# Spreading ScalarE's steps and S's products over each block, and one scratch row for the search, in a graph-attention and nucleus-diffusion kernel

## The chip, the cores and the metric

The kernel runs on one core of a Trainium2 chip. The metric is the device time of one execution in microseconds, as the median over several executions. A core has five engines with a queue each, which run their instructions in the order of the queue and wait for each other by semaphores: PE (TensorE, matrix products), ACT (ScalarE), DVE (VectorE), POOL (GpSimd) and SP (SyncE, which here only issues DMAs).

## The reference, cut to what matters

There are N = 2708 nodes with 512 features each, and a 0/1 adjacency matrix. Layer 0 is a graph attention layer; layer 1 is a diffusion with two steps. Nearly all that the change touches is in layer 1:

```python
S = S + eye(n)                                     # S is the adjacency
Rf = S / clip(S.sum(axis=1, keepdims=True), 1e-12)
Rb = S / clip(S.sum(axis=0), 1e-12)[:, None]
Xf, Xb, Xa = X, X, X
for s in range(2):
    logits = (Xa @ W1) @ W2 @ (Xa @ W3).T          # 2708 x 2708
    A = softmax(logits, with all but the largest entries that
                together hold 0.9 of the row's softmax set to -inf)
    Xf = Rf @ Xf;  Xb = Rb @ Xb;  Xa = A @ Xa
    Z = Z + (Xf @ U1[s] + Xb @ U2[s] + Xa @ U3[s])
Y = X + Z
out = x + (Y - mean) / sqrt(var + 1e-5) * gamma + beta
```

So each step s needs, for every row, a threshold ("nucleus"): the smallest set of largest probabilities that holds 0.9 of the mass. Then come a product of the sparse matrix A with Xa, two products with S, three small products with U1, U2 and U3, and, after the second step, a layer norm of each row.

## The kernel before, in words

**Tiles and blocks.** The 2708 rows are 22 tiles of 128 (the last has 20). Layer 1 goes through them in pairs of tiles (`pairs`, 11 of them, NP = 11). The main loop (L1295 to L1421) runs for each step s over g = -1 to 10; one pass of it is called a block here. Within a block three pairs are in work: pair g is multiplied (PE), pair g+1 is searched for its threshold (DVE), and the logits of pair g+2 are made and exponentiated (PE, ACT). The order on PE, ACT, DVE and SP is the order in which the Python code emits (`tc.manual_schedule`, L1293); nothing is reordered on those four.

**What a block emits, in order.**
1. `lg[g+2].products()` (L510): 24 products of queries and keys in six column chunks per tile, each chunk copied from PSUM into the row buffer `p` by ACT (L520). The PSUM pool `ps_t` has two buffers, so PE can be two chunks ahead of ACT.
2. `search(lg[g+1], ...)` (L594), first half: DVE finds a threshold by rounds of "sum of all p at or above th" (L625, two per round; 2 rounds for s = 0, 4 for s = 1). It starts from sums at three guessed points, `pts`, which ACT and POOL have prepared (next paragraph, `masses`), read at L642.
3. `early()` (L1351), called after the first round: it has DVE take the row maxima `nmx` of pair g+2 (L545), and it fills the list `fills`, steps for ACT that will be handed out later.
4. `late()` (L1359): the PE work of pair g. `diffused` loads what the S products of earlier blocks made. `attended` (L1090) computes A @ Xa in 12 steps, six per tile: PE turns four 128x128 pieces of the kept row `keep[i]` (L1101), ACT copies them out (`at`, L1105), PE multiplies them with the values `va` (L1120). After a tile's last step ACT scales the result into `xa` (L1128). `mixed` (L1139) does the three products with U1, U2, U3 in 12 steps k (L1156, a load of `u_k` each), and `last()` (L1163) copies the two results into `yo` (ACT, L1168), loads `xw` from y_d (SP, L1171) and adds (POOL, L1172).
5. `finish` (L789), the last part of the search of pair g+1: for each of the two tiles DVE writes p below the threshold into `keep[i]` (L796), takes the 8 largest (L798), for s = 1 does both again for the next 8; then it computes the exact cut, writes the kept row into `keep[i]` (`kept_from` L721 for s = 0, `kept_ranked` L726 to L729 for s = 1) and branches on whether ties need more work (L880).

`keep` has two buffers (pool `wide`, L604), one per tile: those that finish(g+1) writes are those that `attended` of pair g reads. So DVE waits at L796 until PE has turned the last piece of that tile.

**The two lists that are handed out in between.** `fills` holds ACT's steps for pair g+2 (`Logits.exp`, L523): `root` and `full` for each tile (two passes of ACT over a row of 2708, L550 and L557), `points` (POOL works out the three guessed points, L562 to L572, and ACT negates them, L569), 12 `look` steps (a pass of ACT over a row each, L550), and `masses` (POOL, L575 to L577). For s = 1 the steps of the layer norm of the pair before (`normed_aside`, L1194) are in the same list: two `mean`, two `spread` (ACT, L1208, and three small POOL operations, L1219 to L1221) and two `ended` (ACT L1208, POOL L1227 and L1228, and a store of `yo` to `out` from POOL's queue, L1229). There are 18 steps for s = 0 and 24 for s = 1.

`others` holds the next products with S (class `Products`, L941). A step is one row block: SP loads `hl` (512 KB) and `s_r` (256 KB) into three buffers each (L971, L973), PE does 8 products (L981 for s = 0, L998 for s = 1). Every 22 such steps are followed by four (`scaled`, L984, or `stored`, L1001) in which ACT copies a result out and issues its store. A block takes 11 or 12 steps for s = 0 and 26 for s = 1 (22 and four `stored`).

**When they are handed out.** `paced(steps, n)` runs the next n of a list. Before the change `attended` runs, from its fourth step on, 2 fills per step up to the ninth and then 1 for s = 0, and 1 per step for the first tile and 2 for the second for s = 1; it runs all of `others` (1 per step) for s = 0, but for s = 1 only 3, in the last steps. `mixed` spreads the remaining `others` over its 12 steps (for s = 1 about 2 each), and takes one fill in six of its steps. What is left of `fills` is run at the end of the block (L1406).

Of the kernel before, what the change touches and what calls it, by code (L numbers as in the profile page):

```python
# [15 lines left out]
OP = mybir.AluOpType  # L16
# [37 lines left out]
def kernel(  # L54
# [25 lines left out]
    KD = D // P  # L80
    NT = -(-N // P)
# [9 lines left out]
    G = 2  # L91
# [502 lines left out]
    def search(lg, looked, early, late):  # L594
# [4 lines left out]
        v = nc.vector  # L599
# [189 lines left out]
        def finish(go):  # L789


            for i, pr in tiles:
                t, m = th[:pr, i:i + 1], kept[:pr, 1, i:i + 1]
                for e in range(0, nx, 8):
                    vs, ss = vn[:pr, i, e:e + 8], sn[:pr, i, e:e + 8]
                    v.scalar_tensor_tensor(keep[i][:pr], ps_[i][:pr], t, ps_[i][:pr], op0=OP.is_lt, op1=OP.mult,  # L796
                                           accum_out=left[:pr, i:i + 1] if e else None)
                    v.max(vs, keep[i][:pr])  # L798
                    if e:
                        m = left[:pr, i:i + 1]  # L800
                        v.tensor_tensor(m, tot[:pr, i:i + 1], m, op=OP.subtract)
                    v.tensor_tensor_scan(ss, vs, vs, m, OP.add, OP.bypass)
                    t = vn[:pr, i, e + 7:e + 8]
            rest = small.tile([P, G, max(NEXT)], F32, name="rest", bufs=1)[:, :, :nx]
            if lg.rank is not None:
                v.tensor_tensor(rest, sn, vn, op=OP.subtract)
                v.tensor_tensor(rest, rest, thr.unsqueeze(2).to_broadcast([P, G, nx]), op=OP.is_lt)
                v.memset(rest[:, :, 0], 1.0)
                v.scalar_tensor_tensor(rest, rest, 0.0, vn, op0=OP.is_equal, op1=OP.add)
                v.tensor_reduce(cut, rest, axis=AX.X, op=OP.min)  # L810

                v.tensor_tensor(rest, vn, cut.unsqueeze(2).to_broadcast([P, G, nx]), op=OP.is_gt)
                v.tensor_mul(rest, rest, sn)
                v.tensor_reduce(top, rest, axis=AX.X, op=OP.max)
                v.tensor_tensor(top, top, kept[:, 1], op=OP.max)
                v.reciprocal(one, cut)
                v.tensor_tensor(room, thr, top, op=OP.subtract)
                v.tensor_mul(room, room, one)
                for x in tiles:
                    kept_ranked(*x)  # L820
                v.memset(flag, 0.0)
                v.tensor_tensor(fr, sn[:, :, nx - 1], thr, op=OP.is_lt)
                v.tensor_mul(fr, fr, thr)
                v.scalar_tensor_tensor(short, fr, 1.0 - 1e-5, den, op0=OP.mult, op1=OP.is_gt)


                v.tensor_scalar(room, room, 0.5, ROUND, op0=OP.add, op1=OP.add)
                v.tensor_scalar(room, room, ROUND, None, op0=OP.subtract)
                v.tensor_tensor(over, den, top, op=OP.subtract)
                v.tensor_mul(over, over, one)  # L830
                v.tensor_tensor(over, over, room, op=OP.subtract)
                v.tensor_mul(over, over, over)
                v.tensor_scalar(over, over, 0.25, None, op0=OP.is_gt)
                return branch(go)
            v.tensor_tensor(fr, sn[:, :, nx - 1], thr, op=OP.is_lt)
            v.tensor_mul(fr, fr, thr)
            v.tensor_tensor(sn, sn, vn, op=OP.subtract)
            v.tensor_tensor(sn, sn, thr.unsqueeze(2).to_broadcast([P, G, nx]), op=OP.is_lt)
            v.memset(sn[:, :, 0], 1.0)

            v.scalar_tensor_tensor(rest, sn, 0.0, vn, op0=OP.is_equal, op1=OP.mult)
            v.scalar_tensor_tensor(sn, sn, 0.0, vn, op0=OP.is_equal, op1=OP.add)
            v.tensor_reduce(cut, sn, axis=AX.X, op=OP.min)
            v.tensor_tensor(rest, rest, cut.unsqueeze(2).to_broadcast([P, G, nx]), op=OP.is_equal)
            v.tensor_reduce(tied, rest, axis=AX.X, op=OP.max)
            for x in tiles:
                kept_from(*x)
            v.memset(flag, 0.0)


            v.scalar_tensor_tensor(short, fr, 1.0 - 1e-5, den, op0=OP.mult, op1=OP.is_gt)
            eighths = vn[:, :, 7:nx:8]
            v.tensor_tensor(eighth, eighths, cut.unsqueeze(2).to_broadcast([P, G, nx // 8]), op=OP.is_equal)
            v.tensor_reduce(fr, eighth, axis=AX.X, op=OP.max)
            v.tensor_scalar(fr, fr, -1e-5, 1.0 + 1e-5, op0=OP.mult, op1=OP.add)
            v.tensor_mul(fr, fr, thr)
            v.tensor_tensor(over, den, cut, op=OP.subtract)
            v.tensor_tensor(over, over, fr, op=OP.is_ge)
            v.tensor_tensor(over, over, tied, op=OP.max)
            branch(go)  # L860
# [41 lines left out]
    with ExitStack() as st:  # L902
# [134 lines left out]
        def paced(steps, n):  # L1037
            for step in steps[:n]:
                step()
            del steps[:n]  # L1040
# [49 lines left out]
        def attended(s, grp, keep, rden, fills, others, then):  # L1090

            def turned(i, t, cs):
                pr = rows[t]
                pt = ps_t.tile([P, TG, P], F32, name="t")
                at = work.tile([P, TG, P], F32, name="at")
                for j, c in enumerate(cs):  # L1100
                    nc.tensor.transpose(pt[:rows[c], j, :pr], keep[i][:pr, cols[c]], ident[:pr, :pr])  # L1101
                full = sum(rows[c] == P for c in cs)
                for r, j0, j1 in ((P, 0, full), (rows[cs[-1]], full, len(cs))):
                    if j0 < j1:
                        nc.scalar.copy(at[:r, j0:j1, :pr], pt[:r, j0:j1, :pr])  # L1105
                return at

            steps = [(i, t, cs) for i, t in enumerate(grp) for cs in tgroups]
            at = turned(*steps[0])
            xa = []  # L1110
            total = len(others)
            for n, (i, t, cs) in enumerate(steps):
                pr = rows[t]
                nxt = turned(*steps[n + 1]) if n + 1 < len(steps) else then()
                if n >= 3:
                    paced(fills, 1 + i if s else 1 if n > 8 else 2)
                if cs[0] == 0:
                    pa = ps_a.tile([P, D], F32, name="a")
                for j, c in enumerate(cs):
                    nc.tensor.matmul(pa[:pr], lhsT=at[:rows[c], j, :pr], rhs=va[:rows[c], c, :],  # L1120
                                     start=(c == 0), stop=(c == NT - 1))
                if not s:
                    paced(others, (total * (1 + i) + 23) // 24)
                elif i and cs[0] >= NT // 2 or len(grp) == 1:
                    paced(others, 1)
                if cs[-1] == NT - 1:
                    xa.append(work.tile([P, D], F32, name="xa"))
                    nc.scalar.activation(xa[i][:pr], pa[:pr], AF.Copy, scale=rden[:pr, i:i + 1])  # L1128
                    if not s:
                        nc.gpsimd.dma_start(out=xa_d[cols[t], :], in_=xa[i][:pr])  # L1130
                at = nxt
            return xa, at
# [6 lines left out]
        def mixed(s, grp, order, v, others, fills):  # L1139
# [5 lines left out]
            def part(n):  # L1145
# [6 lines left out]
                for k in range(KD):  # L1152
                    u_k = up.tile([P, D], F32, name="u_k")
                    nc.sync.dma_start(out=u_k, in_=u[s, k * P:(k + 1) * P, :])
                    for i, t in enumerate(grp):
                        nc.tensor.matmul(pz[i][:rows[t]], lhsT=v_t[:, k, i * P:i * P + rows[t]], rhs=u_k,  # L1156
                                         start=(n == 0 and k == 0), stop=(n == 2 and k == KD - 1))
                    paced(others, -(-len(others) // (3 * KD - n * KD - k)))
                    if n < 2 and k < 3:
                        paced(fills, 1)  # L1160
                return v_t

            def last():  # L1163
# [129 lines left out]
        with tc.manual_schedule(engines={PE, ACT, DVE, SP}):  # L1293
            rest_of_first = []
            for s in range(STEPS):  # L1295
# [37 lines left out]
                for g in range(-1, NP):  # L1333
# [15 lines left out]
                    others = S.take(n) if s or g < 0 else S.splitting(S.take(n), 9)  # L1349

                    def early(g=g):  # L1351
                        sums, squares, ends = normed_aside(norms) if norms else ([], [], [])
                        if g + 2 < NP:
                            steps = lg[g + 2].exp(between=ends)
                            fills.extend(sums + steps[:2] + squares + steps[2:])
                        else:
                            fills.extend(sums + squares + ends)

# [96 lines left out]
```

## Time and profile before

| | |
|---|---|
| runs of the kernel | 3882.49, 3883.42, 3888.15 us; median 3883.42 |
| the profiled execution's own time | 3880.74 us |
| its span, first to last instruction | 3878.8 us |
| blocks of s = 0 (g = 0 to 10), first product with A to the last with U | 1287 to 2412 us from the span's start |
| blocks of s = 1 | 2541 to 3868 us |
| busy in the block of s = 1 from 3179.6 to 3310.6 us (131.0 us) | PE 117.75, DVE 92.61, ACT 64.42, POOL 30.80 us |
| mean granted clock of PE over the span | 0.944 |

Times in the profile are from the span's start; "idle before, releaser" names what ended the idle time of an engine just before an instruction. A line such as "t L518 <- ACT p L520" says that L518 on PE, which writes t, waited for ACT's L520, which writes p. PE counts each of its fp32 products as two records, so an `attended` step shows as x8 at L1120 and an S step of s = 1 as x8 at L998 (which are single records). Layer 0 (to about 1090 us) and the preparation of each step are not touched by the change, apart from the block g = -1.

### The profile page before, as it was taken

How to read it: one execution, taken by the hardware profiler on the slowest of the kernel's cores; microseconds unless marked ns; L12 is line 12 of the kernel's file. 1: busy time of each engine (PE TensorE's matmuls, PEld its weight loads, DVE VectorE, ACT ScalarE, POOL GpSimd, SP SyncE). 2: the span in 40 equal slices, each digit the busy share in tenths (PEclk: the TensorE clock that was granted, in tenths of full speed). 3: DMA queues.
4: the chain of work that ended last, by engine and by line, in shares of the span. 5: the costliest groups of instructions: out<-in, count | busy, mean ns of one | idle time of the engine just before them, and what ended most of it. 6: DMA issues, size and time to landing. Idle time of an engine off the chain costs nothing. (4 is left out here: it accounts for less than half of the span.)

```text
span 3878.8 us, 35347 instructions
## 1 busy us (share of the span) xinstructions
PE 3419.4 (88%) x11058; PEld 1758.6 (45%) x11058; DVE 2634.8 (68%) x4749; ACT 1551.6 (40%) x2387; POOL 898.6 (23%) x1117
## 2 busy tenths in 40 slices
PE   8999999999766898989989897579898989898888
PEld 4333333334444454545544452445554555455543
DVE  4687898999852555556466525996598668766992
ACT  2343211111024655655556412463445444544521
POOL 4115142343310122122112212111123122212231
PEclk9999999999878899999989998889999999999999
DMA  3475423323068555445344453725754574457453
GB/s 112 159 262 203 146 101 118 99 86 111 36 201 293 193 203 202 151 145 177 128 159 163 159 162 112 256 83 195 251 182 149 179 255 165 143 203 246 164 182 110
DMA packets 296045, 644.28 MB, mean 166 GB/s; under 512 B 37804, under 2 KB 87614, under 8 KB 292828
## 3 DMA queue, kind: packets, MB, share of 16 engines
q1 hardware_dynamic: 262596, 550.73, 43.5%
q0 software_dynamic: 20176, 68.11, 4.5%
q10 hardware_dynamic: 13020, 22.63, 1.5%
q8 instruction: 89, 1.46, 0.2%
q14 instruction: 164, 1.34, 0.1%
HBM read 518.78 MB, written 122.57 MB: 165 GB/s over the span
## 5 line engine op out<-in xcount | busy, mean ns | idle before, releaser
L1120 PE MATMUL a<-va,at 128*128 128x512 f32 (+2 forms) x1936 | 910.3, 610 | 50.7 <-ACT at L1105 50.3
L426 PE MATMUL po<-e,fw 128*65 128x512 f32 (+4 forms) x2112 | 842.3, 555 | 29.9 <-DVE e L424 21.2
L424 DVE SCALAR_TENSOR_TENSOR e<-r_b,kk,a_c 128x512 f32<-128x512 f32 (+4 forms) x1056 | 751.1, 739 | 69.0 <-PE po L426 17.8
L550 ACT ACTIVATE junk_a<-p,nth 128x2708 uint8<-128x2708 f32 (+1 forms) x240 | 612.7, 2553 | 5.7 <-ACT xe L1004 0.8
L998 PE MATMUL q<-s_r,hl 128*128 128x512 f32 (+1 forms) x2112 | 549.6, 408 | 63.1 <-DMA s_r<-s_d 57.2
L1156 PE MATMUL a<-u_k,v_t 128*128 128x512 f32 (+1 forms) x1056 | 505.0, 614 | 53.5 <-ACT xa L1128 30.0
L1120 PEld LDWEIGHTS a<-va,at 128*128 128x128 f32 (+2 forms) x1936 | 344.4, 190 | 433.7 <-issue 353.4
L426 PEld LDWEIGHTS po<-e,fw 128*65 128x65 f32 (+1 forms) x2112 | 286.8, 140 | 545.6 <-issue 268.9
L998 PEld LDWEIGHTS q<-s_r,hl 128*128 128x128 f32 x2112 | 380.5, 193 | 232.5 <-issue 95.9
L625 DVE SCALAR_TENSOR_TENSOR junk<-p,th 128x2708 bf16<-128x2708 f32 (+1 forms) x132 | 405.2, 3069 | 4.3
L981 PE MATMUL q<-hl,s_r 128*128 128x512 f32 x968 | 284.1, 437 | 70.1 <-DMA s_r<-s_d 68.1
L1156 PEld LDWEIGHTS a<-u_k,v_t 128*128 128x128 f32 (+1 forms) x1056 | 190.1, 190 | 288.1 <-issue 199.5
L1105 ACT COPY at<-t 128x512 f32<-128x512 f32 (+3 forms) x308 | 139.9, 474 | 440.3 <-PE t L1101 432.9
L518 PE MATMUL t<-keys,q_t 128*128 128x452 f32 x528 | 175.6, 461 | 124.0 <-ACT p L520 102.9
L981 PEld LDWEIGHTS q<-hl,s_r 128*128 128x128 f32 x968 | 183.9, 194 | 161.6 <-issue 86.8
L796 DVE SCALAR_TENSOR_TENSOR keep<-p,th 128x2708 f32<-128x2708 f32 (+1 forms) x44 | 133.5, 3033 | 165.8 <-PE t L1101 164.7
L798 DVE MAX8 vn<-keep 128x8 f32<-128x2708 f32 (+1 forms) x66 | 196.8, 2981 | 2.3
L545 DVE TENSOR_REDUCE nmx<-p 128x1 f32<-128x2708 f32 (+1 forms) x44 | 129.8, 2968 | 86.2 <-ACT p L520 86.2
L518 PEld LDWEIGHTS t<-keys,q_t 128*128 128x128 f32 x528 | 96.4, 220 | 199.0 <-ACT p L520 162.6
L1172 POOL TENSOR_TENSOR yo<-yo,xw 128x512 f32<-128x512 f32 (+1 forms) x22 | 32.6, 1500 | 632.8 <-DMA xt_d<-xe 439.6
L408 ACT ACTIVATE s_c<-a_c 128x512 fp32r<-128x512 f32 (+3 forms) x132 | 76.2, 577 | 247.6 <-DMA a_c<-in_adj_t_dram 120.6
L520 ACT COPY p<-t 128x452 f32<-128x452 f32 (+2 forms) x264 | 134.3, 538 | 84.6 <-PE t L518 68.4
(319 smaller groups left out, 3377.6 us busy)
## 6 DMA issues: line engine op xcount, KB each, us to landing
s_r<-s_d SPq DMA_DIRECT2D x330, 256.0 KB
hl<-vhl_d SPq DMA_DIRECT2D x132, 512.0 KB
u_k<-in_L_gnn_U_dram SPq DMA_DIRECT2D x264, 256.0 KB
hl<-fhl_d SPq DMA_DIRECT2D x132, 512.0 KB
hl<-bhl_d SPq DMA_DIRECT2D x132, 512.0 KB
arow<-in_adj_dram SPq DMA_DIRECT2D x21, 1354.0 KB
s_d<-s_c SPq DMA_DIRECT2D x88, 256.0 KB
a_c<-in_adj_t_dram SPq DMA_DIRECT2D x84, 256.0 KB
```

What stands on the lines that cost most here:

```text
L424: nc.vector.scalar_tensor_tensor(e[:pr, :cw], r_b[:pr, i, :cw], kk[:pr, t, hd:hd + 1], a_c[t][:pr, :cw], op0=OP.max, op1=OP.mult)
L426: nc.tensor.matmul(po[i][:, :cw], lhsT=fw[:pr, t, hd, :], rhs=e[:pr, :cw], start=(t == 0), stop=(t == NT - 1))
L518: nc.tensor.matmul(pl[:, :c1 - c0], lhsT=q[:, i], rhs=self.keys[:, c0:c1], start=(i == 0), stop=(i == 1))
L520: nc.scalar.copy(p[:pr, c0:c1], pl[:pr, :c1 - c0])
L550: nc.scalar.activation(junk[:pr], self.p[i][:pr], func, **kw)
L625: v.scalar_tensor_tensor(junk_b[:pr], ps_[i][:pr], th, ps_[i][:pr], op0=OP.is_ge, op1=OP.mult, accum_out=dst)
L798: v.max(vs, keep[i][:pr])
L981: nc.tensor.matmul(self.half[j], lhsT=s_r[:, j * P:(j + 1) * P], rhs=hl[:, h], start=(c == 0 and h == 0), stop=(c == NT - 1 and h == 1))
L998: nc.tensor.matmul(self.half[k][:, :w], lhsT=hl[:, h, k * P:(k + 1) * P], rhs=s_r[:, :w], start=(c == 0 and h == 0), stop=(c == NT - 1 and ...
L1105: nc.scalar.copy(at[:r, j0:j1, :pr], pt[:r, j0:j1, :pr])
L1120: nc.tensor.matmul(pa[:pr], lhsT=at[:rows[c], j, :pr], rhs=va[:rows[c], c, :], start=(c == 0), stop=(c == NT - 1))
L1156: nc.tensor.matmul(pz[i][:rows[t]], lhsT=v_t[:, k, i * P:i * P + rows[t]], rhs=u_k, start=(n == 0 and k == 0), stop=(n == 2 and k == KD - 1))
```

## The change

Three things are changed.

- **One scratch row.** In `finish` the row of values below the threshold, which is only read by the `max` after it, goes into `keep[0]` for both tiles. The kept rows themselves are still written into `keep[i]` later.
- **S's products.** `attended` hands out one step of `others` after each of its 12 steps, for both s. For s = 0 that is what it did; for s = 1 it means 12 in `attended` and 14 in `mixed`, where it was 3 and 23.
- **ACT's steps.** `attended` hands out one fill per step from the third on (10 in all), `mixed` spreads the rest evenly over its 12 steps. The order in the list changes too: the two `mean` steps come after `points`, and `spread` and `ended` after `masses`, at the list's end. Where there is no norm to do (all blocks of s = 0, and the first of s = 1), two steps that do nothing stand in place of the two `mean` steps. In the block g = -1, which hands out one fill for every two steps of `others`, these empty steps take two of the turns.

```diff
@@ finish
-                    v.scalar_tensor_tensor(keep[i][:pr], ps_[i][:pr], t, ps_[i][:pr], op0=OP.is_lt, op1=OP.mult,
+                    v.scalar_tensor_tensor(keep[0][:pr], ps_[i][:pr], t, ps_[i][:pr], op0=OP.is_lt, op1=OP.mult,
                                            accum_out=left[:pr, i:i + 1] if e else None)
-                    v.max(vs, keep[i][:pr])
+                    v.max(vs, keep[0][:pr])
@@ attended
-            total = len(others)
             for n, (i, t, cs) in enumerate(steps):
                 pr = rows[t]
                 nxt = turned(*steps[n + 1]) if n + 1 < len(steps) else then()
-                if n >= 3:
-                    paced(fills, 1 + i if s else 1 if n > 8 else 2)
+                if n >= 2:
+                    paced(fills, 1)
...
-                if not s:
-                    paced(others, (total * (1 + i) + 23) // 24)
-                elif i and cs[0] >= NT // 2 or len(grp) == 1:
-                    paced(others, 1)
+                paced(others, 1)
@@ mixed
                     paced(others, -(-len(others) // (3 * KD - n * KD - k)))
-                    if n < 2 and k < 3:
-                        paced(fills, 1)
+                    paced(fills, -(-len(fills) // (3 * KD - n * KD - k)))
@@ early
-                        sums, squares, ends = normed_aside(norms) if norms else ([], [], [])
+                        sums, squares, ends = normed_aside(norms) if norms else ([lambda: None] * G, [], [])
                         if g + 2 < NP:
-                            steps = lg[g + 2].exp(between=ends)
-                            fills.extend(sums + steps[:2] + squares + steps[2:])
+                            fills.extend(lg[g + 2].exp(between=sums) + squares + ends)
                         else:
                             fills.extend(sums + squares + ends)
```

In the diff `sums`, `squares` and `ends` are the `mean`, `spread` and `ended` steps.

## The prediction, on record before the changed kernel ran

> **What bounds the kernel now.** I read the page first, then the waits of PE in the blocks of each step, then timelines of single blocks.
>
> ```profile
> span 3878.8 us, 35347 instructions
> PE 3419.4 (88%) x11058; PEld 1758.6 (45%) x11058; DVE 2634.8 (68%) x4749; ACT 1551.6 (40%) x2387; POOL 898.6 (23%) x1117
> ...
> PEclk9999999999878899999989998889999999999999
> ```
>
> PE is busy 88% of the span and no other engine comes near; what a change of order can win is PE's idle time and the slow clock that follows it. The waits of PE from 2600 to 3690 us (most of s = 1), and then from 1290 to 2190 us (s = 0); columns: total us, times, longest.
>
> ```profile
> PE t L518 <- ACT p L520: 52.9, 11, 8.4
> PE a L1120 <- ACT at L1105: 21.0, 10, 3.6
> PE a L1156 <- ACT xa L1128: 20.3, 9, 6.2
> PE q L998 <- DMA s_r<-s_d: 15.7, 25, 2.0
> ```
>
> ```profile
> PE a L1120 <- ACT at L1105: 23.0, 22, 5.5
> ...
> PE t L518 <- ACT p L520: 12.0, 40, 0.7
> PE a L1156 <- ACT xa L1128: 9.7, 8, 2.5
> PE a L1156 <- ACT v_t L1053: 3.6, 2, 2.0
> ```
>
> In both, PE waits for ACT copies, and ACT is late because of `fills` in front of them. The largest, L518, sits at the start of each block of s = 1. ACT and PE there:
>
> ```profile
> 3181.38 1.07 ACT L1168 COPY yo<-a 128x512 f32<-128x512 f32 x2 [0.47 <-PE t L518]
> 3182.34 2.56 ACT L550 ACTIVATE junk_a<-p,nth 128x2708 uint8<-128x2708 f32 x1
> ...
> 3185.03 2.55 ACT L550 ACTIVATE junk_a<-p,nth 128x2708 uint8<-128x2708 f32 x1
> ...
> 3187.58 0.95 ACT L520 COPY p<-t 128x452 f32<-128x452 f32 x2
> ```
>
> ```profile
> 3176.64 3.60 PE L1156 MATMUL a<-u_k,v_t 128*128 128x512 f32 x8
> 3179.67 1.38 PE L518 MATMUL t<-keys,q_t 128*128 128x452 f32 x4
> 3188.14 7.46 PE L518 MATMUL t<-keys,q_t 128*128 128x452 f32 x20 [7.10 <-ACT p L520]
> ```
>
> Two looks left over at the block's end (2.66 us each) hold the copies back until 8.0 us after E, the end of `mixed` (3179.6); PE idles 7.1 us. In the middle of the block:
>
> ```profile
> 3230.24 3.60 PE L1120 MATMUL a<-va,at 128*128 128x512 f32 x8
> 3239.10 5.40 PE L1120 MATMUL a<-va,at 128*128 128x512 f32 x8 [3.19 <-ACT at L1105]
> ```
>
> The same eight products take 5.40 us after the idle time and 3.60 before it; a window over 3239.3 to 3242.7 shows clock 0.50. So a stall of over 2 us costs itself and about 1.8 us more.
>
> **What the Trainium skill says.** "TensorE: Matmul & The Clock Gate", What's actually happening: after an idle window of some 3.4 us the array falls to half rate and is released again after such a window of work. The trace agrees in size (stretches of 0.50 of 3.4 us and multiples), though gaps of 2.5 us are enough here. The same page, Architectural detail: ACT's and DVE's queues are strictly first in, first out; the ACT timeline above shows it. "SBUF — State Buffer", SBUF: two separate sides: a DVE operation with two SBUF inputs and a POOL operation that reads SBUF exclude each other for the whole instruction. The trace agrees: POOL's power takes 0.56 us alone and 3.35 beside L625. "DMA: Bandwidth & Descriptors", Anatomy of one DMA: about 2.0 us plus bytes over 436 GB/s from POOL's queue, so an estimated 2.6 us for the 256 KB of `yo`; the profile's medians are 2.5 us (y_d) and 3.9 us (out), which I use.
>
> **The change, part by part.**
>
> *Scratch row.* DVE's wait at L796 goes away (about 26 us per block of s = 0), but DVE is not late there: no L1101 of s = 0 waits for it. The next thing late for DVE is `masses`. In s = 1 the S steps stretch `attended` from 12 x 3.87 to 12 x (3.87 + 1.84) = 68 us, so without the scratch row the second tile's L796 would have waited some 20 us; with it the first that needs the second buffer is L729, 39 us after the first L796 (3238.2 to 3277.3), by when the last piece is turned. I price it at nothing; the cover is some 30 us between finish and the next block's first L1101.
>
> *Stalls inside the blocks of s = 1.* With one fill (2.66) and one copy (0.58) ACT needs 3.2 us of each 5.7 us step; in `mixed` 9 looks (24 us) lie in 39 us. So the waits on `at` and `xa` go: 21.0 + 20.3, and one of 2.9 at 2573 us outside that window, 44 us. About ten of them exceed 2 us, with their slow clock 10 x 1.8 = 18 us.
>
> *S loads.* `mixed` before asks 2 x 768 KB + 256 KB per 5.4 us (about 330 GB/s) for ten of its steps, after for two. Of the L998 waits, 15.7 in the window and 5.5 after it, I take two thirds: 14 us.
>
> *The end of the block of s = 1.* The two looks go (5.3 us), and a new chain takes their place: `ended` are the last fills, and the copies into `yo` (ACT) now wait for the store of the old `yo`; behind them in ACT's queue stand the L520 copies, for which PE waits. Let T be the end of the last S step; four steps of `mixed` remain, 16 records, 6.9 us, so E = T + 6.9. ACT: copy and issue of `stored` 1.04, square 0.9: T + 1.95. POOL's three operations for it: 1.2 us alone, T + 3.2; if DVE's first two L625 lie there (E is 40 us after `attended` ends; six looks, the v_t copies that wait for PE's fifth step at 18.5, and three looks put masses at about E - 12; 4.8 us of DVE's small operations follow, so they probably do) until T + 7.1, the second tile's until T + 8.3. Then
>
> ```profile
> 3242.48 1.27 POOL L1228 TENSOR_TENSOR yo<-yo,xw 128x512 f32<-128x512 f32 x1
> 3243.71 1.28 POOL L1227 TENSOR_TENSOR yo<-yo,g_b 128x512 f32<-128x512 f32 x1
> 3244.94 0.67 POOL L1229 DMA_DIRECT2D out_dram<-yo  x1
> ```
>
> twice over: 2 x (1.25 + 1.25) and one issue (0.9) to the second store, whose landing takes 2.5. L520 starts at T + 15.0 (E + 8.1) if nothing meets DVE, at T + 17.8 (E + 10.9) if it does; 3.9 for the landing adds 1.4. I take E + 9.8 against E + 8.0: +1.8 us in the eight block starts g = 2 to 9, +14 us. Block g = 1 follows one without norms and wins 2 us.
>
> SP's queue: the `xw` loads from y_d now wait for POOL's L1228; behind them stand the q_t, xb_d, `scales`, `v_t`, `hl` and `s_r` loads. In the block shown `hl` is issued 4 us after the first xb_d load, and its bytes are down about 11 us after it; the first S product of the next `attended` comes 12.8 us after the first L520. The xb_d load moves with that L520, so about 2 us are left. Price: nothing, at most 3 us per block.
>
> *Last pairs.* From g = 8 on DVE decides: finish of pair 9, with ties, ended at 3698.4 and that of pair 10 at 3798.6. Earlier `masses` let DVE start some 8 us earlier, not 18 as PE would: I give back 9 us.
>
> *s = 0.* The 12 looks move from `attended` (2 per step) into `mixed`. Gone: 23.0 + 9.7 + 3.6 + 1.8, less 6.4 (seven `xa` waits of 0.9 that the last step's order keeps) and 3 (the `scaled` copies at 1720 to 1744): 28 us, and six slow-clock stretches, 11 us. New: after `xa` ACT has four looks, two v_t copies and five looks, 1.7 + 9 x 2.67 + 1.05 = 26.8 us after the end of `attended`, whereas PE is ready for the key copies (L162) after 23.9 and L518 needs what follows them. That is 2.9 us, 2.45 after the 0.45 that ACT idles there, and about 0.9 for the clock, nine times: 30 us. Net -9.
>
> *Blocks g = -1.* The empty fills leave two looks more behind ACT's last store: 5.3 us before L520 at 1276.6; at 2531.6 ACT waits 2.8 us for DVE anyway, so 2.6. Together +8.
>
> Sum: -44 - 18 - 14 + 14 - 2 + 9 - 9 + 8 = -56 us. Against the profiled execution: 3880.7 - 56 = 3825. The median of the runs is 3883.4, 2.7 higher: 3827. A difference under 0.2% (8 us) can't be told from no change here.
>
> **Rivals.** (B) The end chain is at its light end (-14) and the looks of s = 0 delay PE half as much (up to -16): 3797 to 3813. For it: DVE's passes may lie just before POOL's work. (C) Waits move without going: the chain at E + 12 to E + 14 (18 to 34 us over eight starts) and S loads up to 2 us late (16) give 3845 to 3876. For it: the median landing of `out` is 3.9, and POOL's L1227 and L1228 took 2.57 and 3.48 us where they met DVE. (D) Slower: the same chain beyond E + 16.8. Without it the sum is -70, over eight starts 8.8 us each, on top of the 8.0 of before; all four POOL operations meeting two-input DVE passes (3 us each, +7), with landings of 3.9, reach E + 19: some 3901. Against it: after the first round DVE reduces (L545, one input) or waits for `p`.
>
> **Chances.** Forecast 0.55 (3815 to 3845), B 0.17, C 0.18, D 0.10. The range 3800 to 3872 leaves out part of B and D. Faster by over 0.2% 0.85, within 0.06, slower 0.09.
>
> **What would show it.** In s = 1: no waits of L1120 on `at` over 1 us; L518 still waiting 6 to 10 us per block, now behind L1168 (the new line of L1168's copy) that waits for the `out` store; DVE's wait at L642 shorter. In s = 0: L162 released late, by ACT itself. Wrong if L518's wait vanishes or exceeds 12 us, if L998 waits at the start of `attended`, or if L1101 waits for DVE in the middle blocks.

## The result, and the profile after

The change gained nothing and cost a little: 3889.72 us median of 20 runs (3881.78 to 3899.36), against 3879.91 us of 20 runs of the kernel before (3870.74 to 3899.82). The ratio is 1.0024, 95% interval 1.0014 to 1.0035, so the kernel became 0.24% slower. The forecast was 3827.

The page after, the span, the busy times and the granted clock:

```profile
span 3880.0 us, 35402 instructions
...
PE 3388.3 (87%) x11058; PEld 1759.7 (45%) x11058; DVE 2655.2 (68%) x4749; ACT 1564.3 (40%) x2387; POOL 868.4 (22%) x1117
...
PEclk9999999999878898999999999889999999999989
```

PE is busy 31 us less than before with the same products, and the span is the same: PE idles that much more. The row of the clock hardly differs; the mean granted clock is 0.938, where it was 0.944. In such a case the page's totals don't say where to look, and the steps have to be compared one by one. Taking each step from its first product with A to its last with U:

| | before | after | forecast for the difference | measured |
|---|---|---|---|---|
| up to the first product of s = 0 and between the steps (g = -1) | 1287, 129 | 1295, 131 | +8 | +10 |
| s = 0 | 1125 | 1162 | -9 | +37 |
| s = 1 | 1327 | 1281 | -55 | -46 |

These sum to +1, and the two profiled spans differ by 1.2 us. The medians differ by 9.8 us; where the rest sits can't be read from one execution of each.

The waits of PE from 2640 to 3690 us after (s = 1; total us, times, longest):

```profile
PE t L518 <- ACT p L520: 78.1, 10, 11.4
PE q L999 <- DMA s_r<-s_d: 7.9, 3, 4.7
...
PE a L1120 <- ACT at L1106: 0.4, 2, 0.2
```

The waits for `at` and `xa` are gone, as forecast, those for S's loads (L999 is the old L998; 15.0 us before in the same window) are halved, and the wait of L518 at the start of each block has grown from 52.9 to 78.1. The end of one block of s = 1 (the old L1168 is L1164, the old L1229 is L1225). In this timeline and those below, lines that don't bear on the argument are left out:

```profile
3324.41 0.67 POOL L1225 DMA_DIRECT2D out_dram<-yo  x1 [0.30 <-POOL yo L1224]
3327.53 0.58 ACT L1164 COPY yo<-a 128x512 f32<-128x512 f32 x1 [4.62 <-DMA out_dram<-yo]
3328.01 0.58 POOL L1225 DMA_DIRECT2D out_dram<-yo  x1 [0.30 <-POOL yo L1224]
3331.21 0.58 ACT L1164 COPY yo<-a 128x512 f32<-128x512 f32 x1 [3.09 <-DMA out_dram<-yo]
3331.69 0.98 ACT L520 COPY p<-t 128x452 f32<-128x452 f32 x2
3332.28 4.24 PE L518 MATMUL t<-keys,q_t 128*128 128x452 f32 x9 [11.06 <-ACT p L520]
```

This is the chain that the prediction drew: each copy into `yo` waits for a store of the old `yo` (3.1 and 3.2 us from issue to release), and the key copies stand behind both. E, the end of L1153's last products, is 3320.4 here, so L520 starts at E + 11.3.

The waits of PE from 1290 to 2230 us (s = 0) are where the loss is:

```profile
PE q L982 <- DMA s_r<-s_d: 59.2, 7, 16.5
PE t L518 <- ACT kq_b L163: 12.0, 6, 2.4
PE a L1153 <- ACT xa L1125: 9.1, 8, 2.1
...
PE a L1120 <- ACT at L1106: 2.0, 5, 1.1
```

The line of L982 was this before:

```profile
PE q L981 <- DMA s_r<-s_d: 13.2, 5, 7.0
```

ACT's waits fell as forecast (L1120 from 23.8 to 2.0 in this window), the key copies are late by some 2 us a block, near the forecast's 2.45, and a wait that the prediction never mentions, for the loads of S's products, went from 13.2 us to 59.2. Where it comes from shows in one block, whose first L518 is at 1503.6:

```profile
1501.44 38.24 SPq L1025 DMA_DIRECT2D split_hl<-xfb_d  x2
1503.68 0.21 POOL L577 TENSOR_TENSOR pts<-signs,above 128x6 f32<-128x6 f32 x1
1512.44 3.04 DVE L625 SCALAR_TENSOR_TENSOR junk<-p,th 128x2708 bf16<-128x2708 f32 x1
1534.93 0.43 DVE L1013 TENSOR_SCALAR split_hl<-split_hl 128x512 int32<-128x512 int32 x1
1536.38 0.54 POOL L1016 DMA_DIRECT2D bhl_d<-split_hl  x1 [24.54 <-DVE split_hl L1015]
1539.74 0.68 SPq L972 DMA_DIRECT2D hl<-vhl_d  x1
1545.44 3.68 PE L982 MATMUL q<-hl,s_r 128*128 128x512 f32 x8 [16.50 <-DMA s_r<-s_d]
```

A function that the text so far left out is at work, `split` (L1009 to L1026). In s = 0 eight steps of `others` in each block also call it: DVE splits the oldest loaded rows into a high and a low part (L1013, L1015), POOL stores them (L1016), and SP loads the next rows into the same pool of two buffers (L1025). The load has to wait for the store of the buffer that it takes. Read the lines downwards: the looks end late, so the masses (L577) are there only at 1503.7; DVE's first round (L625) starts at 1512.4, and the splits, which stand behind both rounds in DVE's queue, at 1534.9; the store goes at 1536.4; and SP only then issues the `hl` and `s_r` loads queued behind it. (The first line covers two loads of L1025: one leaves at once, and the other stands for 37.5 us.) The `hl` and `s_r` loads have nothing to do with the split, and PE waits 16.5 us for them. In the same block before:

```profile
1462.23 0.20 POOL L577 TENSOR_TENSOR pts<-signs,above 128x6 f32<-128x6 f32 x1
...
1478.95 28.60 SPq L1024 DMA_DIRECT2D split_hl<-xfb_d  x2
...
1502.80 0.43 DVE L1012 TENSOR_SCALAR split_hl<-split_hl 128x512 int32<-128x512 int32 x1
...
1513.46 3.75 PE L981 MATMUL q<-hl,s_r 128*128 128x512 f32 x8 [7.01 <-DMA s_r<-s_d]
```

Here the block's L518 began at 1481.1, so the split came 21.7 us into it, against 31.4 after. The other blocks agree: before, the masses come 16 to 19 us ahead of the first L518 of a block, and after, in the eight blocks that follow g = 0, 0.1 to 0.3 us behind it; the first split moves from 21.7 to 31.4 or 31.5 us in five of seven. SP stood still before too, only 9 to 10 us less; most of that was covered by what had already been loaded.

### The profile page after: what moved, and what is told of

Read it like the earlier page. It is cut to its first block, busy times and chain, and to the rows that moved or that the text cites. A ratio compares the mean times of both kernels' runs of the same rounds, so it can differ in the third digit from the quotient of the medians.

```text
span 3880.0 us, 35402 instructions
## 1 busy us (share of the span) xinstructions
PE 3388.3 (87%) x11058; PEld 1759.7 (45%) x11058; DVE 2655.2 (68%) x4749; ACT 1564.3 (40%) x2387; POOL 868.4 (22%) x1117
## 4 chain that ended last, share of the span: by engine, by line
PE 45%; ACT 8%; DMA 8%; issue 5%; POOL 5%; DVE 1%; SPq 1%; ACTq 0%; POOLq 0%; DVEq 0%
PE a L1120 18%; PE q L999 11%; ACT junk_a L550 6%; PE a L1153 5%; PE q L982 5%; DMA s_r<-s_d 4%; PE t L518 3%; PE t L1102 2%; PE po L426 1%; DMA xfb_d<-xe 1%; POOL ln_sums L1216 1%; DMA out_dram<-yo 1%; ACT p L520 1%; DVE junk L625 1%; POOL ln_sums L1215 1%
## 5 line engine op out<-in xcount | busy, mean ns | idle before, releaser
L1120 PE MATMUL a<-va,at 128*128 128x512 f32 (+2 forms) x1936 | 893.9, 601 | 13.8 <-ACT at L1106 13.2
L999 PE MATMUL q<-s_r,hl 128*128 128x512 f32 (+1 forms) x2112 | 574.2, 416 | 61.1 <-DMA s_r<-s_d 55.6
L1153 PE MATMUL a<-u_k,v_t 128*128 128x512 f32 (+1 forms) x1056 | 491.5, 605 | 28.5 <-DMA u_k<-in_L_gnn_U_dram 18.0
L1120 PEld LDWEIGHTS a<-va,at 128*128 128x128 f32 (+2 forms) x1936 | 339.7, 188 | 382.3 <-issue 338.8
L999 PEld LDWEIGHTS q<-s_r,hl 128*128 128x128 f32 x2112 | 380.4, 191 | 245.3 <-issue 116.0
L625 DVE SCALAR_TENSOR_TENSOR junk<-p,th 128x2708 bf16<-128x2708 f32 (+1 forms) x132 | 402.8, 3052 | 4.3
L982 PE MATMUL q<-hl,s_r 128*128 128x512 f32 x968 | 287.9, 442 | 115.8 <-DMA s_r<-s_d 115.6
L518 PE MATMUL t<-keys,q_t 128*128 128x452 f32 x528 | 182.9, 479 | 167.4 <-ACT p L520 133.5
L1153 PEld LDWEIGHTS a<-u_k,v_t 128*128 128x128 f32 (+1 forms) x1056 | 189.0, 187 | 265.7 <-issue 201.6
L982 PEld LDWEIGHTS q<-hl,s_r 128*128 128x128 f32 x968 | 186.8, 197 | 209.1 <-issue 123.4
L545 DVE TENSOR_REDUCE nmx<-p 128x1 f32<-128x2708 f32 (+1 forms) x44 | 129.4, 2967 | 148.1 <-ACT p L520 148.1
L518 PEld LDWEIGHTS t<-keys,q_t 128*128 128x128 f32 x528 | 101.8, 230 | 245.4 <-ACT p L520 200.5
L642 DVE TENSOR_TENSOR pts<-top,pts 128x6 f32<-128x6 f32 x22 | 5.5, 251 | 276.8 <-POOL pts L577 276.8
L520 ACT COPY p<-t 128x452 f32<-128x452 f32 (+2 forms) x264 | 136.7, 539 | 84.6 <-PE t L518 68.7
L1102 PE MATMUL t<-ident,keep 128*128 128x128 f32 (+1 forms) x968 | 148.4, 274 | 15.6 <-DVE keep L748 11.4
```

The source lines that it names most:

```text
L518: nc.tensor.matmul(pl[:, :c1 - c0], lhsT=q[:, i], rhs=self.keys[:, c0:c1], start=(i == 0), stop=(i == 1))
L520: nc.scalar.copy(p[:pr, c0:c1], pl[:pr, :c1 - c0])
L625: v.scalar_tensor_tensor(junk_b[:pr], ps_[i][:pr], th, ps_[i][:pr], op0=OP.is_ge, op1=OP.mult, accum_out=dst)
L982: nc.tensor.matmul(self.half[j], lhsT=s_r[:, j * P:(j + 1) * P], rhs=hl[:, h], start=(c == 0 and h == 0), stop=(c == NT - 1 and h == 1))
L999: nc.tensor.matmul(self.half[k][:, :w], lhsT=hl[:, h, k * P:(k + 1) * P], rhs=s_r[:, :w], start=(c == 0 and h == 0), stop=(c == NT - 1 and ...
```

## The experiments

Ratios are to the kernel before, with 95% intervals; s = 0 and s = 1 are measured as in the table above (before 1125 and 1327, after 1162 and 1281).

**1. s = 0 as before.** The changed kernel, with the old places of the fills in s = 0:

```diff
@@ attended
-                if n >= 2:
-                    paced(fills, 1)
+                if n >= (2 if s else 3):
+                    paced(fills, 1 if s or n > 8 else 2)
@@ mixed
-                    paced(fills, -(-len(fills) // (3 * KD - n * KD - k)))
+                    if s:
+                        paced(fills, -(-len(fills) // (3 * KD - n * KD - k)))
+                    elif n < 2 and k < 3:
+                        paced(fills, 1)
@@ early
-    sums, squares, ends = normed_aside(norms) if norms else ([lambda: None] * G, [], [])
+    sums, squares, ends = normed_aside(norms) if norms else ([lambda: None] * G if s else [], [], [])
```

> The changed kernel with the fills of s = 0 placed as before (three steps late and up to two per step in attended, three in mixed, no empty steps); s = 1 and the scratch row stay as changed. Theory 1 (the loss is s = 0's late looks: masses late, DVE's splits late, SP's queue behind them): s = 0 falls from 1162 to about 1125 us again, the waits of L982 in it from 59 to under 20 us, the whole to 3835 to 3850, about 1% faster than before. Rival (s = 0 loses by the one scratch row or by what s = 1's changes do to the prologue and the loads): s = 0 stays near 1160 us and the whole near 3890.

3832.22 us, ratio 0.9877 (0.9858 to 0.9897). s = 0 took 1114 us, s = 1 1284, and L982's waits are back at 13.4 us. The loss is in s = 0 and in the places of its fills. (s = 0 is 11 us shorter than before; one L998 wait of 5.5 us near its end is missing. It may be the scratch row; this was not separated.)

**2. s = 0 alone.** The kernel before, with only s = 0's part of the change; in `early` the empty steps and the order of the list as well.

```diff
@@ attended
-                if n >= 3:
-                    paced(fills, 1 + i if s else 1 if n > 8 else 2)
+                if n >= (3 if s else 2):
+                    paced(fills, 1 + i if s else 1)
@@ mixed
-                    if n < 2 and k < 3:
+                    if not s:
+                        paced(fills, -(-len(fills) // (3 * KD - n * KD - k)))
+                    elif n < 2 and k < 3:
                         paced(fills, 1)
```

> The kernel before with the new places of s = 0's fills alone (spread over attended and mixed, and the empty steps); s = 1 and two scratch rows as before. Theory 1: s = 0 loses 35 to 45 us by itself, with 5 more in the block g = -1: 3920 to 3935, about 1.1% slower than before. Rival (the loss needs the one scratch row or s = 1's part): within 10 us of before, 3875 to 3893.

3928.36 us, ratio 1.0123 (1.0105 to 1.0141); s = 0 1166 us, L981's waits 58.4 us. The loss needs neither the scratch row nor s = 1.

**3. The split's load from POOL's queue.** The changed kernel with

```diff
@@ split
-                    nc.sync.dma_start(out=hl[:pr, 1], in_=xfb_d[i, cols[t], :])
+                    nc.gpsimd.dma_start(out=hl[:pr, 1], in_=xfb_d[i, cols[t], :])
```

> The changed kernel, only that the load of the split's second half is issued from POOL's queue and no longer from SP's, so that SP's loads of keys and factors need not stand behind a split that DVE has not finished. Theory 1 with SP's queue as the last link: the waits of L982 on s_r in s = 0 fall from 59 us to under 20, and s = 0 by 30 to 45 us, the whole to 3845 to 3860. Rival (the products of S wait because the split's own parts come late, not because SP is blocked; then it does not matter who issues the load): L982 keeps some 50 to 60 us of waits and the time stays within 10 us of 3890.

3819.18 us, ratio 0.9848 (0.9831 to 0.9865), better than expected: s = 0 took 1093 us, 69 less than in the changed kernel and 32 less than before. The waits of PE from 1290 to 2230 us in this kernel:

```profile
PE a L1120 <- ACT at L1106: 15.1, 10, 6.3
PE t L518 <- ACT kq_b L163: 11.6, 7, 2.4
PE a L1153 <- ACT xa L1125: 9.8, 8, 2.5
```

No L982 wait is listed, although masses and splits are as late as in the changed kernel (in the block with L518 from 1490.1, the split is at 1521.6, 31.5 us into it). So the products did not need what was late; SP's queue was the link. What the new key-copy delay costs is seen undisturbed here: 12 us of waits, where the forecast's 30 had 22 of waits (nine of 2.45) and 8 of slow clock.

**4. Norm steps before the looks.** The changed kernel with

```diff
@@ early
-                            fills.extend(lg[g + 2].exp(between=sums) + squares + ends)
+                            fills.extend(lg[g + 2].exp(between=sums + squares + ends))
```

> The changed kernel, only that squares and ends of the norms stand directly behind the sums among the fills of s = 1 and the last looks come after them. Theory 2 (what is left of the wait of L518 in s = 1, 78 us from 2640 to 3690, is the chain store of yo, POOL, ACT's copy at the block's end): the waits of L518 there fall under 30 us and s = 1 by 35 to 60 us, the whole to 3830 to 3855. Rival (the looks at the end take its place, as in the kernel before where two left-over looks held the copies 8.0 us): L518 keeps 60 us or more and the time stays within 15 us of 3890; a third way, masses come later and DVE decides the blocks of s = 1, would show DVE waits at L1102 and a time above 3890.

3850.64 us, ratio 0.9932 (0.9914 to 0.995); s = 1 fell to 1243 us and L518's waits to 31.7 us, 4.2 per block. The chain over the store of `yo` was the residue in s = 1; what now ends the wait is the last look, still on ACT when the block ends.

**5. Both edits**, the diffs of runs 3 and 4, on the changed kernel.

> The changed kernel with both edits that each helped: the split's second load issued from POOL's queue (alone it gave 3819) and squares and ends directly behind the sums (alone 3851, that is 39 us under the changed kernel). If the two causes are separate, one in s = 0 and one in s = 1, the gains add: 3819 - 39 = 3780, range 3772 to 3790, about 2.6% faster than before. If they share a wait (POOL's queue, which then carries both the split's loads and the norms' work), half of the second gain is lost: 3795 to 3815.

3780.8 us, ratio 0.974 (0.9727 to 0.9753); s = 0 1091, s = 1 1242. The two causes are separate and add up.

**6. The split's load from POOL's queue in the kernel before**, the diff of run 3.

> The kernel before, only that the split's second load is issued from POOL's queue. Theory (SP's queue behind DVE's split is a cost in the kernel before too, but a small one: 13.2 us of L981 and 5.5 of L998 waits from 1290 to 2230 us, with slow clock after them): s = 0 wins 15 to 25 us, the whole 3858 to 3868, so that the new fills' own cost in s = 0, with SP freed, would be near nothing. Rival 1 (the late looks cost s = 0 by ACT as well, by the predicted 30 us, and the freed SP merely hides that): the kernel before wins as much from this edit as the changed one did, 60 to 75 us, to 3808 to 3823. Rival 2 (SP's blocks are covered in the kernel before): 3878 to 3888.

3879.1 us, ratio 0.9994 (0.9985 to 1.0003): no gain, the time that the second rival gave. The profile does not show it as cover, though: L981's wait on `s_r` is gone here too (13.2 us before), and L1120's wait for ACT rose from 23.8 to 44.8 us, the longest 10.3. A wait changed its place. Together with runs 1 to 3 this makes a square for s = 0, but the scratch rows differ in it:

| s = 0, us | two rows | one row |
|---|---|---|
| load on SP, old fills | 1125 | 1114 (run 1) |
| load on SP, spread fills | 1166 (run 2) | 1162 |
| load on POOL, old fills | 1125 (run 6) | not run |
| load on POOL, spread fills | not run | 1093 (run 3) |

With the load on SP, spreading ACT's steps costs 41 us with two rows and 48 with one. With the load on POOL it goes with a gain of 32 us, of which up to 11 may be the one row's; the two corners that would tell were not run.

**7. Two scratch rows.** The changed kernel with

```diff
@@ finish
-                    v.scalar_tensor_tensor(keep[0][:pr], ps_[i][:pr], t, ps_[i][:pr], op0=OP.is_lt, op1=OP.mult,
+                    v.scalar_tensor_tensor(keep[i][:pr], ps_[i][:pr], t, ps_[i][:pr], op0=OP.is_lt, op1=OP.mult,
...
-                    v.max(vs, keep[0][:pr])
+                    v.max(vs, keep[i][:pr])
```

> The changed kernel with a row of keep for each tile again in the search's last part, as before; all fills as changed. Theory (the one row is worth nothing, as the prediction priced it): 3882 to 3897. Rival (in s = 1 the second tile's products of L797 now wait some 20 us for the last pieces of the block, and DVE's rounds and splits come later by a part of it): 3900 to 3930, with waits of DVE at L797.

3893.4 us, ratio 1.0034 (1.0022 to 1.0045): the same as the changed kernel. DVE does wait at L797 again (90.0 us from 2640 to 3690 us), but its waits for ACT's p (L545, 103.2 to 66.6) and for the masses (L642, 52.8 to 5.4) shrink by 84. With these fills, and the split's load on SP, the row is worth nothing, as forecast.

**8. No empty steps in the blocks g = -1**, on top of run 5.

```diff
@@ early
-    sums, squares, ends = normed_aside(norms) if norms else ([lambda: None] * G, [], [])
+    sums, squares, ends = normed_aside(norms) if norms else ([lambda: None] * G if g >= 0 else [], [], [])
```

> The changed kernel with both edits of the fifth run, and without the empty steps in the blocks g = -1 of both s; they stay in the blocks of s = 0 with g of 0 and more. Theory (the empty steps leave more looks behind the start, which the prediction priced at 8 us): 6 to 12 us under the fifth run, 3768 to 3775 if that gives 3780. Rival (the start waits for DVE's or POOL's own work, not for ACT's looks): within 3 us of the fifth run.

3772.28 us, ratio 0.9727 (0.9714 to 0.974), 8.5 us under run 5: the size that the prediction gave the empty steps. The two profiled executions show where: s = 0 starts 14 us earlier (1287 against 1301) and is itself 8 us longer (1099 against 1091), so a part of what the start wins is lost again. This is the best version of the study, 2.7% faster than before.

**9. DVE later, ACT untouched.** The kernel before, with four more passes in s = 0, whose sums nothing uses:

```diff
@@ search, ahead of the first use of the masses
+        if looked and not s:
+            pause = vec("pause")
+            for _ in range(2):
+                for i, pr in tiles:
+                    mass(i, pr, lg.pts[:pr, 0, 2, i:i + 1], pause[:pr, i:i + 1])
```

> The kernel before with all its fills in their old places, and four more passes of the kind of L625 (about 3.1 us each, 12.5 us a block) on DVE in s = 0, directly behind its wait for the masses; what they add up is not used. It makes DVE's splits of s = 0 as late as they are in the changed kernel (9 us against the block), with nothing changed on ACT. Theory (late masses matter through DVE's splits and SP's queue behind them): waits of L981 in s = 0 rise from 13 to 40 us or more, s = 0 loses 30 to 45 us, the whole 3910 to 3925. Rival (late looks hurt s = 0 through ACT, not through DVE, which idles 45% of s = 0): within 8 us of 3880.

3957.97 us, ratio 1.0199 (1.0182 to 1.0217), twice the expected loss. s = 0 took 1202 us (1288 to 2490), the waits of the old L981 went from 13.2 to 74.2 us, those of the old L998 from 5.5 to 16.3, while L1120's stayed at 24.2. DVE was then busy 76.0 us in a block of 116 us, so DVE's own load isn't the bound. Late splits alone make a loss of this kind. The size was underestimated: in five of seven blocks the first split is 34.9 to 36.3 us behind the first L518, against 31.4 or 31.5 in the changed kernel. That a slow clock after the waits (0.93 over that block) adds the rest is likely and was not separated.

**10. DVE later, and the split's load from POOL's queue**, the diffs of runs 9 and 3 on the kernel before.

> The same four passes, in the kernel before with the split's second load issued from POOL's queue (the sixth run, 3879). Theory: with SP free, DVE's lateness has no way to PE: no L981 waits over 15 us in s = 0, 3872 to 3890. Rival (SP is not the link; late splits hold the products back by their own data, or late rounds hold back L1101): as much loss as without the free SP, 3910 to 3925.

3929.94 us, ratio 1.012 (1.0104 to 1.0137). Neither expectation: the waits for `s_r` are gone, as the theory had it, and yet 46 us are lost in s = 0, now at L1120, which waits 92.6 us for `at`. The timeline of one such stall (lines of this kernel: L1020 is POOL's store of the split, L1029 the load, L1110 the copy `at`, L1125 the product with it):

```profile
1427.84 0.54 POOL L1020 DMA_DIRECT2D bhl_d<-split_hl  x1 [39.23 <-DVE split_hl L1019]
...
1444.16 1.08 POOL L562 TENSOR_TENSOR x<-sums,powers 128x4 f32<-128x4 f32 x1
1448.79 0.21 ACT L569 ACTIVATE nth<-th_a 128x6 f32<-128x6 f32 x1 [23.08 <-POOL th_a L568]
1452.15 0.57 ACT L1110 COPY at<-t 128x512 f32<-128x512 f32 x1
1452.78 3.78 PE L1125 MATMUL a<-va,at 128*128 128x512 f32 x4 [21.05 <-ACT at L1110]
```

POOL stands at the late split's store, and then at its loads; `points` (L562) queues behind them, ACT's `nth` waits for `points`, ACT's copy of `at` queues behind `nth`, and PE waits for that. The blocked queue moved from SP to POOL. It fits that run 6 gained nothing (ACT's waits at L569 rose there from 34.7 to 53.7 us, with L1120's). In run 3 they are longer still, 68.1 us, and cost PE little. The likely reason is that the spread leaves ACT behind by fewer looks, each of 2.7 us, when `points` comes at last; that was not tried by itself.

**11. S's products late in s = 1**, on top of run 1.

```diff
@@ attended
-                paced(others, 1)
+                if not s or i and cs[0] >= NT // 2 or len(grp) == 1:
+                    paced(others, 1)
```

> The first run's kernel (s = 0 as before, s = 1 as changed, 3832), only that in s = 1 the products of S stand again in the last steps of attended and in mixed; ACT's steps stay spread. The prediction gave the spread of the products 14 us of s = 1's gain and ACT's steps the rest. Theory (as predicted, a small share; the looks carry the gain): L999 waits return to about 16 to 20 us and the whole to 3840 to 3855. Rival (the products are the larger part, as they give ACT's copies more time per step of attended): 3860 to 3885, with waits of L1120 back over 10 us.

3879.3 us, ratio 0.9985 (0.9975 to 0.9995): 47 us above run 1, the rival. s = 1 takes 1322 us here, 5 less than before, against 1284 in run 1: spreading ACT's steps alone wins next to nothing in s = 1. From its first product to the end of pair 7 it takes away the waits for `xa` (18.8 us before, none listed here), pays as much at L518 (46.8 before, 67.9 here), and leaves the waits for `at` (20.3 before, 16.6 here). The gain needs the products spread too. Whether they would win as much with ACT's steps in their old places was not run. Six blocks take 798 us here and 757 in run 1. Of the 41 us, 16 are L1120's waits for `at` (16.1 against 0.4), 7.5 L999's waits for loads (10.1 against 2.6), 2 L518's, and 16 PE's busy time (704.7 against 688.7 for the same products).

**12. ACT's steps done two steps before the end of `mixed` in s = 1**, on top of run 8.

```diff
@@ mixed
-                    paced(fills, -(-len(fills) // (3 * KD - n * KD - k)))
+                    paced(fills, -(-len(fills) // max(3 * KD - (2 if s else 0) - n * KD - k, 1)))
```

> The eighth run's kernel (3772, the best so far), only that in s = 1 the fills are paced to end two steps before the end of mixed. Theory (what is left of the wait of L518 in s = 1, 30 us in eight blocks, is the last look still running on ACT when the block ends): L518 falls under 12 us, 15 to 25 us are won, 3747 to 3758. Rival (the steps run closer in mixed then delay ACT's copies of v_t and xa, or L520 waits for the turned q_t and not for a look): 3765 to 3785.

3793.36 us, ratio 0.9765 (0.975 to 0.9781): 21 us worse than run 8, and by neither expectation's path. L518's waits fell (29.8 to 18.9; 2.3 to 2.8 us at each block start, where run 8 has 4.2, so the last look was a part of them), but L999 now waits 43.9 us instead of 11.6. One block's start in this kernel:

```profile
3242.56 3.03 DVE L625 SCALAR_TENSOR_TENSOR junk<-p,th 128x2708 bf16<-128x2708 f32 x1
3244.07 6.64 POOL L1168 TENSOR_TENSOR yo<-yo,xw 128x512 f32<-128x512 f32 x2 [6.38 <-ACT yo L1164]
3246.76 4.30 SPq L1198 DMA_DIRECT2D xw<-xb_d  x2
3253.31 0.85 SPq L972 DMA_DIRECT2D hl<-fhl_d  x1
3262.67 3.75 PE L999 MATMUL q<-s_r,hl 128*128 128x512 f32 x8 [5.26 <-DMA s_r<-s_d]
```

and in run 8's:

```profile
3230.97 2.50 POOL L1168 TENSOR_TENSOR yo<-yo,xw 128x512 f32<-128x512 f32 x2 [0.73 <-ACT yo L1164]
3232.27 1.55 SPq L1198 DMA_DIRECT2D xw<-xb_d  x2
3236.07 0.62 SPq L972 DMA_DIRECT2D hl<-fhl_d  x1
```

The earlier masses let DVE's first passes start 1.5 us ahead of POOL's two additions, which take 6.64 us instead of 2.50; SP's `xw` loads wait for the buffers that the additions read, and the `hl` loads behind them leave 8.3 us after L518 goes on (3244.97) instead of 4.2 (3231.87). The other blocks agree. Of the first eight blocks of s = 1 here, the additions meet DVE's passes in seven and take 6.6 to 7.1 us, and an L999 wait of 3.8 to 5.9 us follows; in the one where they take 2.52 us, it is 0.7. In run 8 they meet only in the first block (6.81 us, a wait of 4.9); in the other seven they take 2.5 us, and the waits are at most 2.6.

## Why the prediction was wrong, point by point

**The step that failed: s = 0.** "The 12 looks move from `attended` (2 per step) into `mixed`" was priced at ACT only: 28 + 11 us gone, 30 us new, net -9. Measured +37. The gone part happened, and the new delay of the key copies was over-priced (12 us of waits, six or seven of about 2 us, not nine of 2.45 with 0.9 of slow clock each). What was left out is the other reader of the last look: the masses, for which DVE waits, with the splits behind DVE's rounds, the store behind the splits, SP's load behind the store, and every load of S's products behind that. The masses came 16 to 19 us later against the block, the first split up to 9.8 us, and PE's waits for the loads grew by 46 us (13.2 to 59.2). Runs 1 and 2 show that the fills of s = 0 make the loss, run 9 that lateness on DVE alone is enough, and run 3 that SP's queue carried it to PE. The prediction did use an idle DVE as its argument ("DVE is not late there: no L1101 of s = 0 waits for it"). That looked at one consumer of DVE. In the waits of SP before, from 1290 to 2330 us, the link was visible (first line; the second is the same wait after, to 2230 us):

```profile
SPq L1024 <- DMA bhl_d<-split_hl: 156.5, 12, 27.9
SPq L1025 <- DMA bhl_d<-split_hl: 201.9, 15, 37.5
```

**s = 1, the sum.** Forecast -55, measured -46. The waits for `at` and `xa` went (41 us; forecast 44 with one outside the window), and PE was busy 15.7 us less in six blocks for the same 2329 records (704.7 to 689.0; forecast 18 for the slow clock). S's loads gave 7.1 us from 2640 to 3690 us, where 14 was forecast for all of s = 1. Behind that window the changed kernel has a new wait of 8.8 us for `at`, at 3702.6, where ACT's copy stands behind a copy into `yo` that waits for its store. The price per stall, "over 2 us costs itself and about 1.8 us more", is a fair estimate and no sharp limit: from 1285 us on before, 32 of 35 idle gaps of PE of 2 us or more lead into a stretch at clock 0.50 within 4 us, and so do 5 of the 8 gaps between 1.5 and 2 us.

**s = 1, the end chain.** The mechanism was right, the size too small: L520 at E + 11.3, not E + 9.8, and L518's waits +25 us, not +14. "If DVE's first two L625 lie there" was weighed at about half; they did lie there in the block shown (3313.6 to 3319.6), and POOL's two small operations took 2.56 and 3.38 us beside them, against 0.19 and 0.55 for the next tile. Six of the eight waits were 10.7 to 11.4 us long, so the heavy case was the rule. Run 4 takes the chain away and wins 38 us in s = 1.

**s = 1, whose gain it is.** The prediction booked the 44 us to ACT's steps ("ACT needs 3.2 us of each 5.7 us step") and gave the products 14. The 5.7 is 3.87 plus the product of S, so the sum had the products in it. Run 11 corrects this: ACT's steps alone take away the waits for `xa`; those for `at` and most of the slow clock go only with the products spread as well. Why a step without its product still waits was not followed up.

**Last pairs.** Forecast +9 given back. Not seen: the lead was 41 us at pair 8's first product and 46 at the end, though PE waits 11.4 us for DVE there, where it was 7.5. In run 8 DVE does hold the last blocks: PE waits 21.7 and 10.2 us for it, and the lead stays at 83 us from pair 8's first product to the end.

**The rest.** The scratch row at nothing: right with the new fills (run 7), open with the old (run 1). The prediction's "about 26 us per block of s = 0" at L796 is a misreading: 26.4 is the longest of eleven waits from 1290 to 2230 us, which sum to 140.0. The empty steps at 8 us: right (+10 in the two starts, 8.5 in run 8). "SP's queue ... at most 3 us per block" held in most blocks of the changed kernel's s = 1, but waits of L999 of 4.7 and 2.3 us stand early in `attended` of two blocks up to 3690 us, at 2713 and 2967 (the prediction's own sign of being wrong there), and run 12 shows how little cover was left.

**The rivals.** None had this loss. D, the slower case, looked for it in the chain at the end of s = 1, which stayed under its point of E + 16.8.

## What to carry to other kernels

When a step moves later, list every reader of its last result and follow each one through the queue that it stands in, including queues that only issue DMAs. A load that waits for a buffer holds back all loads behind it on its queue (37.5 us in the block shown), and an engine that is idle 45% of the time (DVE, busy 549 of 1000 us in s = 0 before) can still be the one that frees that buffer. Where two changes meet in a queue, try all four combinations, with everything else equal: here spreading ACT's steps cost 41 to 48 us or went with a gain of 32, depending on whose queue carried one load.

## What the runs showed of the hardware that was not expected

The queues that issue DMAs kept their order as an engine's does. In the changed kernel one load on SP's queue that waited 37.5 us for its buffer held loads that did not need it, and with that load on POOL's queue their 59.2 us of waits on PE were gone (run 3). On POOL's queue the late split held POOL's arithmetic, which held ACT, which held PE for 21.05 us (run 10). "SBUF — State Buffer", SBUF: two separate sides, says that a DVE operation with two SBUF inputs and a POOL operation that reads SBUF exclude each other; run 12 agrees and has the price for a moved start: two additions of 2.50 us together took 6.64 when DVE's pass had started 1.5 us earlier.
